# A gated recurrence of 512 steps: the direct x products moved into step 0, the block products moved by one step

## The chip, the cores and the metric

The kernel runs on one core of one Trainium2 chip. The time is the device time of one execution in microseconds, from the core's first instruction to its last with what the runtime lays around it; the shown runs of the kernel before took 1656.86, 1657.39 and 1657.92 us (median 1657.39). The core has a matrix engine (PE, with weight loads as a row of their own, PEld), a vector engine (DVE), an activation engine (ACT), a general engine (POOL) and a queue that issues transfers (SP).

## The reference

Eight sequences of 512 steps and 512 features go through a gated recurrence, and the input is added to its result. For each step t, with a state `h` of 8 x 512:

```python
fused = sigmoid(concat([x_t, h]) @ w_W + w_b)
hidden_state, output_state = split(fused, 2)
memory_state = x_t @ wx_W + wx_b + hidden_state * (h @ wh_W + wh_b)
h = output_state * h + (1 - output_state) * tanh(memory_state)
out[t] = x_t + h
```

Everything is float32. Of each step's products the part with `x_t` (512 x 1536) doesn't depend on the state and can be done at any time before the step; the part with `h` (512 x 1536) can only start when the step before is done.

## The kernel before, in words

**Layout.** The 512 features are cut into four parts of 128; a matmul takes 128 rows of the contraction and writes 32 rows of PSUM (tile "128*32"), so that four matmuls, j = 0 to 3, fill the 128 rows of a bank. Weights are moving operands: `wx` (x part), `wa` and `wb` (state part).

**A step** (one turn of the loop over i, 0 to 511). The state's halves lie in `hTA` (parts k = 0, 1) and `hTB` (k = 2, 3). PE adds the state's products to three banks: A (192 columns: gate r, gate z and the inner product h of half A), B (128) and C (64, in the tile `cs`). The order is the string `ORDER` for all steps but the first, which has `FIRST`; an `x` in it stands for a fourth of a group's x products. When A is complete DVE transposes it (`tr`, `md1A`, `tz`), ACT applies the sigmoids, DVE's scans form the memory, ACT its tanh, and DVE's next scans (`update`) write the new `hTA`; with B and C the same happens for half B. After C, PE does x products that belong to later steps, until the new `hTA` lets the next step's A begin.

**Groups and blocks.** Four steps are a group, two groups a block of eight steps; u = 0 to 7 is a step's place in its block. The x products of groups 0 to 3 are done directly by `prefill` (16 matmuls of 384 columns a group, one part of four matmuls for each k), into `xps[0]` (even groups) or `xps[1]` (odd groups), which `seed` has filled with the bias. From the third block on, the x products of a block are done as seven smaller products (P1 to P7 and a copy E of P5) of sums of weights (`tw`, made by `weight_sum` on DVE) and of sums of x (`sx`, made by `x_sum` on POOL). `x_step` hands out their columns: `SHARE[u]` columns at place u, 384 or 288, in the order of `SLOTS`. The registers AL, BE, GA, DE (halves of `xps`) and `eps` take the products; ACT and DVE copy and add them into `even` and `odd`, from which `spread` (ACT) fills the banks A, B, C of the group and `turn_x` (DVE) its part of `md1`. All of that is written at the end of a step, after its updates, and runs on ACT and DVE while PE does the next step's A.

**The order** of every engine's instructions is that of the program text; a queue waits in front of the instruction whose semaphore isn't there yet. Two banks of each name alternate between groups.

**Around step 0.** SP issues `wx` in four transfers, `wa` in four, `wb` in two, then the second half of x chunk 0 (`load_x(0, 1)`) and chunks 1 to 3. PE does group 0, then a matmul of zeros over `xps[1]` (`warm`), then step 0, whose A products are added onto `xps[0]` itself. DVE's order there is two weight sums of 128 x 1536, then `turn_x(0)`, then step 0's transposes.

Of the kernel before, what the change touches and what calls it, by code (L numbers as in the profile page):

```python
# [16 lines left out]
B = 8  # L17
# [7 lines left out]

ORDER = "A0 B0 A1 A2 A3 B1 B2 B3 C0 C1 C2 C3"

FIRST = "A0 x A1 x A2 x A3 B0 B1 B2 B3 C0 C1 C2 C3"

BANKS = {"A": 192, "B": 128, "C": 64}  # L30

# [22 lines left out]
def tile_cond_rnn_residual(  # L54
# [70 lines left out]
    def load_x(c, half=slice(0, 2)):  # L125

        if c < NCH:
            if c not in xins:
                xins[c] = xin_p.tile([P, 2, NQ, TC * B // 2], F32, tag="xin", name=f"xin_{c}")
            nc.sync.dma_start(  # L130
                out=xins[c][:, half], in_=x[c].rearrange("p (e k n) -> p e k n", e=2, k=NQ)[:, half]
            )
# [18 lines left out]
    wa = const.tile([P, NQ, NQ, 192], F32, name="wa")  # L151
    for k in range(NQ):
        nc.sync.dma_start(out=wa[:, k], in_=wa_d[k])
    wb = const.tile([P, NQ, NQ, 192], F32, name="wb")
    nc.sync.dma_start(out=wb[:, :3], in_=wb_d)
    nc.sync.dma_start(out=wb[:, 3], in_=wb3_d)
# [4 lines left out]
    load_x(0, 1)  # L161

    def pair(n, name, rows, slots):

# [51 lines left out]
    def mm(out_, lhsT, rhs, start=False):  # L216
        nc.tensor.matmul(  # L217
            out_, lhsT, rhs, start=start, stop=False, skip_group_check=True
        )
# [4 lines left out]
    def warm():  # L224

        mm(xps[1], zeros[:, :128], zeros)
# [25 lines left out]
    def seed(g):  # L252

        nc.scalar.copy(xps[g % 2], bias)  # L254

    def prefill(g):

        c, t0 = divmod(g * GS, TC)
        for k in range(NQ):
            for j in range(NQ):  # L260
                mm(
                    xps[g % 2][32 * j : 32 * j + 32, XC],
                    x_of(c, k, t0, GS),
                    wx[:, k, j, :],
                )
            yield
# [5 lines left out]
    def spread(g, names):  # L272

        for n in names:
            nc.scalar.copy(banks[g % 2][n], source(g)[:, XP[n]])

    def turn_x(g, hf):

        c0 = XP["X"].start + HU * hf
        nc.vector.transpose(  # L280
            md1[hf][g % 2][:, :, :, 1].rearrange("p n c -> p c n"), source(g)[:, c0 : c0 + HU]
        )
# [11 lines left out]
    def weight_sum(n, k=slice(0, 2), j=slice(0, 2)):  # L294

        a, b = [
            (wx_of(0, 1), wx_of(0, 0)),
            (wx_of(1, 1), tw[0]),
            (wx_of(1, 1), wx_of(0, 1)),
            (wx_of(1, 0), tw[1]),  # L300
        ][n]
        nc.vector.tensor_tensor(tw[n][:, k, j], a[:, k, j], b[:, k, j], ALU.subtract)
# [55 lines left out]
    weight_sum(0)  # L358
    spread(0, "BCA")
    for hf in range(2):  # L360
        turn_x(0, hf)

    pool_done = {}
    for i in range(T):
# [7 lines left out]

        for n in (ORDER if i else FIRST).split():
            if n == "x":
                take(first[1], 1)
                continue
            bank, k = n[0], int(n[1])
            hs = hT[k // 2][i % NH][:, :, k % 2, 2]
            for j in range(NQ):
                to = ps[bank] if i or bank != "A" else xps[0][:, XP["A"]]  # L380
                mm(to[32 * j : 32 * j + 32, :], hs, wh(bank, k, j))
# [87 lines left out]
        if i == 0:  # L469

            seed(2)
# [16 lines left out]
        o, u = divmod(i, 2 * GS)  # L488
        nxt, two = o + 1 < NG // 2, o + 2 < NG // 2
        if i == 0:  # L490
            nc.scalar.copy(odd[:, XC], xps[1][:, XC])
        if u == 0:
            spread(2 * o + 1, "AC")
            turn_x(2 * o + 1, 0)
            turn_x(2 * o + 1, 1)
        elif u == 1:
            if o and nxt:
                nc.vector.tensor_tensor(reg(GA), reg(BE), more[HI], ALU.add)
                nc.scalar.copy(even[LO, XC], reg(AL))
            spread(2 * o + 1, "B")  # L500
        elif u == 2:
            if o == 0:
                nc.scalar.copy(even[:, XC], xps[0][:, XC])
                seed(3)
            elif nxt:
# [4 lines left out]
        elif u == 3:  # L510
            if two:
                nc.scalar.copy(reg(AL), bias[LO, XC])
                x_sum(o + 2, 0)
        elif u == 4:
            if o == 0:
                nc.scalar.copy(odd[:, XC], xps[1][:, XC])
            elif nxt:
# [3 lines left out]
        elif u == 5 and nxt:  # L521
            if o:
                nc.scalar.copy(odd[LO, XC], reg(GA))
            spread(2 * o + 2, "A")
            turn_x(2 * o + 2, 0)
        elif u == 6 and nxt:
            spread(2 * o + 2, "BC")
            turn_x(2 * o + 2, 1)
            if two:
                nc.scalar.copy(more[HI], eps)  # L530
                x_sum(o + 2, 1)
        elif u == 7 and nxt:
            if two:
                nc.scalar.copy(reg(BE), reg(AL))
                nc.scalar.copy(both[LO], reg(DE))
                x_sum(o + 2, 3)
        if 1 <= i < 9:
            weight_sum(1 if i < 5 else 3, *divmod((i - 1) % 4, 2))
        if i == 2:
# [102 lines left out]
```

## Time and profile before

| | |
|---|---|
| time, median of 3 runs | 1657.39 us |
| profiled execution: its time, its span | 1659.38 us, 1657.43 us |
| mean granted TensorE clock | 0.999 |
| matmul records | 54253 |
| busy: PE, PEld, DVE, ACT, POOL | 1645.1, 1487.9, 1152.0, 1198.4, 303.2 us |
| moved by DMA | 31.16 MB |

PE's busy time counts pipelined matmuls whose ends are modelled, so a busy share of 99% doesn't say that PE has no slack; it is read from the distance between matmuls. One matmul of the program appears as two records in the trace, so "x8" is four matmuls. The bank A of step 0 is called xp in the trace of before, since it is the tile `xps[0]`. The start of a step is the first row `A<-wa,hTA`, or the row `tr<-A` of DVE, the first reader of a complete A.

### The profile page before, as it was taken

How to read it: one execution, taken by the hardware profiler on the slowest of the kernel's cores; microseconds unless marked ns; L12 is line 12 of the kernel's file. 1: busy time of each engine (PE TensorE's matmuls, PEld its weight loads, DVE VectorE, ACT ScalarE, POOL GpSimd, SP SyncE). 2: the span in 40 equal slices, each digit the busy share in tenths (PEclk: the TensorE clock that was granted, in tenths of full speed). 3: DMA queues.
4: the chain of work that ended last, by engine and by line, in shares of the span. 5: the costliest groups of instructions: out<-in, count | busy, mean ns of one | idle time of the engine just before them, and what ended most of it. 6: DMA issues, size and time to landing. Idle time of an engine off the chain costs nothing.

```text
span 1657.4 us, 126070 instructions
## 1 busy us (share of the span) xinstructions
PE 1645.1 (99%) x54253; PEld 1487.9 (90%) x54253; DVE 1152.0 (70%) x9193; ACT 1198.4 (72%) x6009; POOL 303.2 (18%) x1283
## 2 busy tenths in 40 slices
PE   8999999999999999999999999999999999999998
PEld 5999999999888889999999999999999999989987
DVE  5776676676766766767667667676676676766766
ACT  4777777777777777777777777777777777777775
POOL 1211111111111111111111111111111111111111
PEclk9999999999999999999999999999999999999999
DMA  4000000000000000000000000000000000000000
GB/s 182 11 14 17 15 14 15 17 15 14 14 16 16 14 14 16 16 14 14 16 16 14 15 16 16 15 14 16 16 15 14 16 16 15 14 16 11 10 10 10
DMA packets 37287, 31.16 MB, mean 19 GB/s; under 512 B 4084, under 2 KB 35060, under 8 KB 36600
## 3 DMA queue, kind: packets, MB, share of 16 engines
q1 hardware_dynamic: 36576, 22.95, 4.5%
q8 instruction: 424, 6.95, 1.7%
q14 instruction: 135, 1.11, 0.2%
q10 hardware_dynamic: 152, 0.16, 0.0%
HBM read 14.70 MB, written 8.39 MB: 14 GB/s over the span
## 4 chain that ended last, share of the span: by engine, by line
PE 98%; DVE 1%; DMA 1%; issue 0%; ACT 0%; SPq 0%
PE A L217 40%; PE B L217 26%; PE xp L217 17%; PE cs L217 13%; PE eps L217 1%; DMA wx<-in_wx_dram 1%; DVE tr L407 0%; DVE m L391 0%; DVE tz L407 0%; DVE md1B L423 0%; DVE hTA L391 0%; DVE md1A L423 0%; SPq L149 0%; ACT hTB L246 0%; ACT xp L254 0%
## 5 line engine op out<-in xcount | busy, mean ns | idle before, releaser
L217 PE MATMUL A<-wa,hTA 128*32 128x192 f32 x8176 | 547.6, 326 | 2.1 <-DVE hTA L391 2.1
L217 PE MATMUL A<-wa,hTB 128*32 128x192 f32 x8176 | 440.7, 326 | 0.0
L217 PE MATMUL B<-wb,hTA 128*32 128x128 f32 x8192 | 440.6, 273 | 0.0
L217 PEld LDWEIGHTS A<-wa,hTA 128*32 128x32 f32 x8176 | 281.3, 122 | 129.8 <-DVE hTA L391 103.7
L407 DVE STREAM_TRANSPOSE tr<-A 128x64 f32<-128x64 f32 x511 | 127.6, 250 | 369.4 <-PE A L217 369.4
L545 POOL TENSOR_TENSOR ot<-xin,hTB 128x16 f32<-128x16 f32 x503 | 125.9, 250 | 1309.3 <-DVE hTB L391 989.0
L217 PEld LDWEIGHTS B<-wb,hTA 128*32 128x32 f32 x8192 | 337.5, 122 | 5.7
L217 PEld LDWEIGHTS A<-wa,hTB 128*32 128x32 f32 x8176 | 323.0, 122 | 13.0 <-DVE hTB L391 0.4
L217 PE MATMUL B<-wb,hTB 128*32 128x128 f32 x8192 | 332.2, 273 | 0.0
L217 PE MATMUL xp<-tw,sx 128*32 128x96 f32 x1488 | 267.5, 433 | 0.0
L217 PEld LDWEIGHTS B<-wb,hTB 128*32 128x32 f32 x8192 | 255.1, 122 | 0.0
L246 ACT ACTIVATE md0A<-tr 128x16 f32<-128x16 f32 x512 | 112.3, 219 | 191.3 <-DVE tr L407 177.4
L391 DVE TENSOR_TENSOR_SCAN hTB<-hd0B,hTB 128x24 f32<-128x24 f32 x1024 | 157.8, 195 | 100.5 <-ACT hTB L246 100.5
L217 PE MATMUL cs<-wb,hTA 128*32 128x64 f32 x8192 | 222.9, 219 | 0.0
L217 PE MATMUL cs<-wb,hTB 128*32 128x64 f32 x8192 | 222.8, 219 | 0.0
L217 PE MATMUL xp<-wx,xin 128*32 128x384 f32 (+2 forms) x1304 | 219.6, 425 | 0.0
L217 PEld LDWEIGHTS cs<-wb,hTA 128*32 128x32 f32 x8192 | 200.4, 122 | 0.0
L391 DVE TENSOR_TENSOR_SCAN hTA<-hd0A,hTA 128x24 f32<-128x24 f32 x1024 | 190.1, 186 | 0.0
L246 ACT ACTIVATE hd0B<-tz 128x16 f32<-128x16 f32 x512 | 116.0, 227 | 93.3 <-DVE tz L407 93.3
L246 ACT ACTIVATE hTB<-hTB 128x16 f32<-128x16 f32 x512 | 120.1, 234 | 78.9 <-DVE hTB L391 53.1
L217 PEld LDWEIGHTS cs<-wb,hTB 128*32 128x32 f32 x8192 | 173.0, 122 | 0.0
L246 ACT ACTIVATE hTA<-m 128x8 f32<-128x8 f32 x1024 | 160.6, 206 | 2.8 <-DVE m L391 0.5
(105 smaller groups left out, 2664.3 us busy)
## 6 DMA issues: line engine op xcount, KB each, us to landing
out_dram<-ot SPq DMA_DIRECT2D x128, 64.0 KB, 1.6
xin<-in_x_dram SPq DMA_DIRECT2D x112, 64.0 KB, 2.2
wx<-in_wx_dram SPq DMA_DIRECT2D x4, 768.0 KB, 6.9
wa<-in_wa_dram SPq DMA_DIRECT2D x4, 384.0 KB, 8.9
wb<-in_wb_dram SPq DMA_DIRECT2D x1, 1152.0 KB
xin<-in_x_dram SPq DMA_DIRECT2D x3, 256.0 KB, 8.3
wb<-in_wb_dram SPq DMA_DIRECT2D x1, 384.0 KB, 11.2
head<-in_xh_dram ACTq DMA_DIRECT2D x1, 144.0 KB, 4.9
```

The source lines that it names most:

```text
L217: nc.tensor.matmul(out_, lhsT, rhs, start=start, stop=False, skip_group_check=True)
L246: inst = nc.scalar.activation(out_, in_, func, **kw).ins
L391: return nc.vector.tensor_tensor_scan(*[t_[:, :, c_].rearrange("p n c s -> p (n c s)") for t_ in (out_, d0, d1)], 0.0, ALU.mult, ALU.add,).ins
L407: inst = nc.vector.transpose(t_.rearrange("p c n -> p (c n)"), raw[n][hf]).ins
L545: return engine.tensor_tensor(ot[:, t, 2 * hf : 2 * hf + 2, :].rearrange("p c n -> p n c"), x_of(c, slice(2 * hf, 2 * hf + 2), t, 1).rearr ...
```

## The change

- `FIRST`: in step 0 the four A parts come first, then four x parts, then B and C. The x parts are those of group 2, not of group 1.
- All of group 1 is done before the loop, where the `warm` matmul stood. Step 0's A goes to the bank A, not to `xps[0]`; `spread(0)` copies A first.
- Group 3 is done one part a step in steps 1 to 4; before, groups 2 and 3 were done two parts a step there.
- `weight_sum(2)` stands behind `turn_x(0)`, and `weight_sum(0)` in step 0 between the first half's memory scans and `turn_r(1)`. The seeds of groups 2 and 3 and the copy of group 1 into `odd` stand ahead of the loop.
- The second half of x chunk 0 is issued ahead of `wb`, not behind it.
- The block products start at place u = 5 of the block two before theirs, not at 4: `SHARE` and the sums and copies at the end of each step are turned by one place. Exceptions: `more<-eps` moves from u = 6 to u = 1 of the next block, `spread(2o+1, "AC")` from 0 to 1 and its "B" from 1 to 2, `spread(2o+2)` from A at 5 and BC at 6 to AB at 6 and C at 7, `turn_x(2o+1)` stays at u = 0.

```diff
-FIRST = "A0 x A1 x A2 x A3 B0 B1 B2 B3 C0 C1 C2 C3"
+FIRST = "A0 A1 A2 A3 x x x x B0 B1 B2 B3 C0 C1 C2 C3"
-SHARE = [384, 384, 384, 288, 288, 288, 288, 384]
+SHARE = [384, 384, 384, 384, 288, 288, 288, 288]
...
+    load_x(0, 1)
     wb = const.tile([P, NQ, NQ, 192], F32, name="wb")
...
-        at = sum((SHARE * 2)[4 : u if u > 3 else u + 8]) - SHARE[4] // 3
-        o += 2 if u > 3 else 1
+        at = sum((SHARE * 2)[5 : u if u > 4 else u + 8]) - SHARE[5] // 3
+        o += 2 if u > 4 else 1
...
     take(prefill(0))
-    warm()
-    first = {g: prefill(g) for g in (1, 2, 3)}
-    weight_sum(2)
-    weight_sum(0)
-    spread(0, "BCA")
+    take(prefill(1))
+    first = {g: prefill(g) for g in (2, 3)}
+    spread(0, "ABC")
     for hf in range(2):
         turn_x(0, hf)
+    weight_sum(2)
+    seed(2)
+    nc.scalar.copy(odd[:, XC], xps[1][:, XC])
+    seed(3)
...
-                take(first[1], 1)
+                take(first[2], 1)
...
-        if i < 5:
-            take(first[(i + 3) // 2], 2)
-        if i > 3:
+        if 1 <= i < 5:
+            take(first[3], 1)
+        if i > 4:
             x_step(*divmod(i, 2 * GS))
...
-        pa = ps["A"] if i else xps[0][:, XP["A"]]
+        pa = ps["A"]
...
         memory(0, 1)
+        if i == 0:
+            weight_sum(0)
         turn_r(1)
...
         if u == 0:
-            spread(2 * o + 1, "AC")
+            if o == 0:
+                spread(1, "A")
+            if sums:
+                nc.scalar.copy(reg(BE), reg(AL))
+                nc.scalar.copy(both[LO], reg(DE))
+                x_sum(o + 1, 3)
             turn_x(2 * o + 1, 0)
             turn_x(2 * o + 1, 1)
         elif u == 1:
-            if o and nxt:
+            if sums:
+                nc.scalar.copy(more[HI], eps)
+            spread(2 * o + 1, "BC" if o == 0 else "AC")
```

PE from the end of group 0 to the B products of step 0, as a difference (`xp_183` is `xps[0]`, `xp_184` is `xps[1]`, `A_179` the first A bank; `head` holds x of groups 0 and 1, `xin` the second half of chunk 0):

```order
-L217 MATMUL xp_184<-zeros 128x512
-L217 MATMUL xp_183<-wa,hTA_90 32x192 x4
-L217 MATMUL xp_184<-wx,head 32x384 x4
-L217 MATMUL xp_183<-wa,hTA_90 32x192 x4
-L217 MATMUL xp_184<-wx,head 32x384 x4
-L217 MATMUL xp_183<-wa,hTB_98 32x192 x4
-L217 MATMUL xp_184<-wx,head 32x384 x4
-L217 MATMUL xp_183<-wa,hTB_98 32x192 x4
+L217 MATMUL xp_184<-wx,head 32x384 x16
+L217 MATMUL A_179<-wa,hTA_90 32x192 x8
+L217 MATMUL A_179<-wa,hTB_98 32x192 x8
+L217 MATMUL xp_183<-wx,xin_85 32x384 x16
```

Sixteen matmuls of group 1 stand ahead of step 0's first A product, and sixteen of group 2 between its A and B products.

DVE from the head of the loop to the transposes for half B in step 0, first before (`tw_161` and `tw_159` are two of the summed weights):

```order
L302 TENSOR_TENSOR tw_161<-wx 128x1536
L302 TENSOR_TENSOR tw_159<-wx 128x1536
L280 STREAM_TRANSPOSE md1A_110<-xp_183 128x64
L280 STREAM_TRANSPOSE md1B_112<-xp_183 128x64
L407 STREAM_TRANSPOSE tr_0_294<-xp_183 128x64
```

and now:

```order
L280 STREAM_TRANSPOSE md1A_110<-xp_183 128x64
L280 STREAM_TRANSPOSE md1B_112<-xp_183 128x64
L302 TENSOR_TENSOR tw_161<-wx 128x1536
L408 STREAM_TRANSPOSE tr_0_311<-A_179 128x64
L424 STREAM_TRANSPOSE md1A_110<-A_179 128x64
L408 STREAM_TRANSPOSE tz_0_315<-A_179 128x64
L434 MEMSET idle 128x1
L392 TENSOR_SCALAR m_0_309<-md0A_106,md1A_110 128x16 x2
L302 TENSOR_TENSOR tw_159<-wx 128x1536
L408 STREAM_TRANSPOSE tr_0_324<-B_180 128x64
```

The readers of `xps[0]` no longer stand behind the two weight sums, and the second of these stands inside step 0 (scans appear as TENSOR_SCALAR here).

ACT between the last state copy of one step and the first sigmoid of the next, at the place with the most copies: before at u = 6,

```order
L246 ACTIVATE hTB_105<-hTB_105 128x8x2
L275 COPY B_180<-even 128x128
L275 COPY cs<-even 128x64
L530 COPY more<-eps 64x384
L246 ACTIVATE md0A_107<-tr_39_3895 128x2x8
```

and now at u = 1:

```order
L246 ACTIVATE hTB_100<-hTB_100 128x8x2
L504 COPY more<-eps 64x384
L275 COPY A_181<-odd 128x192
L275 COPY cs<-odd 128x64
L246 ACTIVATE md0A_106<-tr_42_4160 128x2x8
```

The copy of `eps` stands with the spread of another group, 192 and 64 columns in place of 128 and 64.

More of the change, by code (lines that the diff above doesn't have):

```diff
@@ L159, in wh @@
         return wa[:, k, j] if bank == "A" else wb[:, k, j, {"C": slice(0, 64), "B": slice(64, 192)}[bank]]
-    load_x(0, 1)
     def pair(n, name, rows, slots):
@@ L379, in tile_cond_rnn_residual @@
             for j in range(NQ):
-                to = ps[bank] if i or bank != "A" else xps[0][:, XP["A"]]
-                mm(to[32 * j : 32 * j + 32, :], hs, wh(bank, k, j))
-        if i < 5:
-            take(first[(i + 3) // 2], 2)
-        if i > 3:
+                mm(ps[bank][32 * j : 32 * j + 32, :], hs, wh(bank, k, j))
+        if 1 <= i < 5:
+            take(first[3], 1)
+        if i > 4:
             x_step(*divmod(i, 2 * GS))
@@ L468, in tile_cond_rnn_residual @@
         tc.add_manual_dep(update(0, 1), r_done[1].name, SYNC)
-        if i == 0:
-            seed(2)
         if i == T - 1:
@@ L490, in tile_cond_rnn_residual @@
         if i == 0:
-            nc.scalar.copy(odd[:, XC], xps[1][:, XC])
+            nc.scalar.copy(even[:, XC], xps[0][:, XC])
+        sums = o > 0 and nxt
         if u == 0:
-            spread(2 * o + 1, "AC")
+            if o == 0:
[4 more added lines that the diff above has]
+                x_sum(o + 1, 3)
             turn_x(2 * o + 1, 0)
@@ L496, in tile_cond_rnn_residual @@
         elif u == 1:
-            if o and nxt:
+            if sums:
+                nc.scalar.copy(more[HI], eps)
+            spread(2 * o + 1, "BC" if o == 0 else "AC")
+        elif u == 2:
+            if sums:
                 nc.vector.tensor_tensor(reg(GA), reg(BE), more[HI], ALU.add)
                 nc.scalar.copy(even[LO, XC], reg(AL))
[L500 to L505, printed above, removed]
+            if o:
+                spread(2 * o + 1, "B")
+        elif u == 3:
+            if sums:
                 nc.vector.tensor_tensor(odd[HI, XC], reg(GA), both[LO], ALU.add)
@@ L509, in tile_cond_rnn_residual @@
                 x_sum(o + 2, 2)
-        elif u == 3:
+        elif u == 4:
+            if o == 0:
+                nc.scalar.copy(odd[:, XC], xps[1][:, XC])
             if two:
@@ L513, in tile_cond_rnn_residual @@
                 x_sum(o + 2, 0)
[L514 to L517, printed above, removed]
+        elif u == 5:
+            if sums:
                 nc.vector.tensor_tensor(even[HI, XC], reg(BE), both[HI], ALU.add)
@@ L520, in tile_cond_rnn_residual @@
                 nc.scalar.copy(reg(DE), step_bias[HI])
-        elif u == 5 and nxt:
+        elif u == 6 and nxt:
+            spread(2 * o + 2, "AB")
+            turn_x(2 * o + 2, 0)
+        elif u == 7 and nxt:
             if o:
                 nc.scalar.copy(odd[LO, XC], reg(GA))
[L524 to L527, printed above, removed]
+            spread(2 * o + 2, "C")
             turn_x(2 * o + 2, 1)
             if two:
-                nc.scalar.copy(more[HI], eps)
                 x_sum(o + 2, 1)
[L532 to L536, printed above, removed]
         if 1 <= i < 9:
```

## The prediction

> **What bounds the kernel now.** I read the page's busy times and chain first, then the distances between matmuls (timeline of PE), since a busy share of a pipelined engine doesn't show slack, and last the first 22 us engine by engine.
>
> ```profile
> PE 1645.1 (99%) x54253; PEld 1487.9 (90%) x54253; DVE 1152.0 (70%) x9193; ACT 1198.4 (72%) x6009; POOL 303.2 (18%) x1283
> PE 98%; DVE 1%; DMA 1%; issue 0%; ACT 0%; SPq 0%
> ...
> 47.64 0.55 PE L217 MATMUL A<-wa,hTA 128*32 128x192 f32 x8
> 50.26 0.49 PE L217 MATMUL xp<-wx,xin 128*32 128x384 f32 x2
> 50.91 0.55 PE L217 MATMUL A<-wa,hTA 128*32 128x192 f32 x8
> 57.44 0.55 PE L217 MATMUL A<-wa,hTA 128*32 128x192 f32 x8
> 60.54 0.55 PE L217 MATMUL A<-wa,hTA 128*32 128x192 f32 x8
> ...
> 1644.38 0.55 PE L217 MATMUL A<-wa,hTA 128*32 128x192 f32 x8 [0.23 <-DVE hTA L391]
> 1647.46 0.55 PE L217 MATMUL A<-wa,hTA 128*32 128x192 f32 x8 [0.24 <-DVE hTA L391]
> ```
>
> Step starts give three lengths. A step's state products take 47.64 to 50.26, 2.62 us. With 384 columns of block products the step is 3.27 us (47.64 to 50.91), with 288 it is 3.10 (57.44 to 60.54), without any 3.08 (1644.38 to 1647.46): there PE waits for the new state, 0.46 us in all. So up to 0.46 us of x products are free in a step, and every microsecond above that is paid in full. Steps with products are bound by PE, the last steps by the chain through DVE and ACT.
>
> The start is another matter. PE there, with what DVE does beside it:
>
> ```profile
> 11.15 0.85 PE L217 MATMUL xp<-wx,head 128*32 128x384 f32 x8 [0.48 <-DMA wx<-in_wx_dram]
> 11.94 1.13 PE L217 MATMUL xp<-zeros 128*128 128x512 f32 x2
> 15.05 0.86 PE L217 MATMUL xp<-wa,hTA 128*32 128x192 f32 x8 [1.99 <-issue]
> ...
> 19.66 0.52 PE L217 MATMUL xp<-wa,hTB 128*32 128x192 f32 x8
> 19.99 0.64 PE L217 MATMUL B<-wb,hTA 128*32 128x128 f32 x16
> 20.86 0.42 PE L217 MATMUL cs<-wb,hTA 128*32 128x64 f32 x16
> ...
> 21.31 0.84 PE L217 MATMUL xp<-wx,head 128*32 128x384 f32 x8
> 21.95 0.52 PE L217 MATMUL A<-wa,hTA 128*32 128x192 f32 x8
> 11.23 3.43 DVE L302 TENSOR_TENSOR tw<-wx 128x1536 f32<-128x1536 f32 x2 [2.01 <-DMA wx<-in_wx_dram]
> 14.74 0.21 DVE L280 STREAM_TRANSPOSE md1B<-xp 128x64 f32<-128x64 f32 x1
> ```
>
> Step 0's A begins at 15.05, 0.10 us after the second transpose of `xps[0]` ends (14.95). That transpose stands behind two weight sums of 3.43 us, and A adds onto the tile which it reads: DVE's order holds PE, not a load. The loads agree:
>
> ```profile
> 3.03 3.46 SPq L153 DMA_DIRECT2D wa<-in_wa_dram  x4
> DMA to landing us min/median/max: 8.3/8.9/9.4
> 7.37 0.33 SPq L156 DMA_DIRECT2D wb<-in_wb_dram  x1
> wb<-in_wb_dram SPq DMA_DIRECT2D x1, 384.0 KB, 11.2
> 9.27 4.03 SPq L130 DMA_DIRECT2D xin<-in_x_dram  x4
> xin<-in_x_dram SPq DMA_DIRECT2D x1, 128.0 KB, 9.7
> ```
>
> The first part of `wa` lands by 3.03 + 9.4 = 12.43 at the latest, the fourth, whose issue ends at 6.49, by 14.8 with the shortest time of that row, 15.4 with its median and 15.9 with the longest; the last of `wb` at 18.57; the x half at 18.97.
>
> Behind the gap PE is slow. Mean clock granted (the column behind the busy time), a microsecond a row:
>
> ```profile
> core 0: us, PE busy (x), PEclk, DMA share, GB/s
> 15.00:16.00 1.00, 0.95 (x12) 0.56 1.00 424
> 16.00:17.00 1.00, 1.00 (x12) 0.50 0.93 393
> 17.00:18.00 1.00, 1.00 (x16) 0.50 0.94 376
> 18.00:19.00 1.00, 1.00 (x16) 0.73 1.06 398
> ```
>
> The missing shares add up to 0.44 + 0.50 + 0.50 + 0.27 = 1.71 us of PE time. The same from the matmuls: at full clock four matmuls of 384 columns take 21.31 to 21.95, 0.645, and four of 192 columns 19.66 to 19.99, 0.325. A with three x parts is 4 x 0.325 + 3 x 0.645 = 3.24; it took 15.05 to 19.99, 4.94.
>
> **The change, part by part.**
>
> *Group 1 ahead of the loop, `warm` and the gap gone.* Group 0's last part begins at 11.15 and ends its work at 11.80. Group 1 needs nothing new (x in `head`, `wx` complete): 4 x 0.645 = 2.58, to 14.38. A now goes to the bank A and waits for one copy by ACT, over by then, and for `wa`: to 14.38 + 1.30 = 15.68. Its fourth part is wanted at 15.36; the longest landing, 15.9, would cost 0.5, the median, 15.4, costs nothing, and I take the median. PE is busy from 11.15 on, so I expect no half clock.
>
> *Group 2 between A and B.* It needs `seed(2)` on ACT, which waits for `turn_x(0)` on DVE, now free at about 12.1 (two transposes of 0.21 us each, as in the row at 14.74, then one copy of 512 columns, which I bound by twice the 0.47 us of 384 columns in the second rival's rows): ready by 14. It needs the x half, now issued ahead of `wb`: 128 KB at about 410 GB/s (last column above) is 0.31 us behind `wa`, so 15.7 with the median and 16.2 with the longest landing, against 15.68. It takes 2.58, to 18.26. In exchange `wb` is 0.31 us later: its last part takes the place of the x half, 18.97. B's last four matmuls want it at 18.26 + 0.65 = 18.91. I price that at 0.1; at worst, `wb` half a microsecond late, 0.5. B 0.87, C 0.45: C ends at 19.68.
>
> *Weight sums.* One takes half of 3.43, 1.72. The first stands at about 12.6 to 14.4 and A's first transpose comes at 15.9. The second begins when half A's scans are done, some 0.8 us behind that (16.8), and ends at 18.5; half B's transposes can't start before B is complete, 19.2. Both lie beside group 2 and cost nothing; if group 2 weren't there, the second would hold `update(0, 0)` and so step 1 by about 1.7.
>
> *Step 1 to 5.* With nothing between C and the next A step 0 closes like the last steps, with 0.46 of waits: step 1 starts at 20.14. Steps 1 to 4 do 2.62 + 0.645 = 3.27 each: step 5 starts at 33.22. Before:
>
> ```profile
> 33.97 0.51 PE L217 MATMUL A<-wa,hTA 128*32 128x192 f32 x8
> 35.74 0.25 DVE L407 STREAM_TRANSPOSE tr<-A 128x64 f32<-128x64 f32 x1 [0.78 <-PE A L217]
> 39.95 0.25 DVE L407 STREAM_TRANSPOSE tr<-A 128x64 f32<-128x64 f32 x1 [1.63 <-PE A L217]
> ```
>
> A step's first transpose comes 35.74 - 33.97 = 1.77 behind its start, so step 5 started at 39.95 - 1.77 = 38.18. Step 4 took 4.21: half a group (1.29) and the first 192 columns of E (0.32). These columns go into step 5, where 0.32 is under the free 0.46, so that step takes 3.08.
>
> *All other steps.* From step 6 on step i does what step i - 1 did. The products end one step later, so of the last steps at 3.08 one is lost, and step 5 is the one gained: zero. Sums and copies keep their distance to the products, or have more; they are hidden behind the next step's A as before, but for the place in the second rival.
>
> Sum: 38.18 - 33.22 = 4.96 us. The same by terms: from 11.80 to 15.05 nothing was done but `warm`, 3.25; half clock 1.71; E 0.32; in steps 1 to 4 of before 0.27 of waits (38.18 - 21.95 = 16.23, against 4 x 3.91 + 0.32); less the 0.46 at the end of step 0 and the 0.1 for `wb`. Group 2's 2.58 us only change their place: into a stretch that starts that much earlier. The span 1657.43 becomes 1652.5. The profiled execution took 1659.38, its median unprofiled 1657.39; I take the difference over: 1657.39 - 4.96 = 1652.4.
>
> **The clock, by row and by rule.** The rows show half clock from 15.1 to about 18.5 after PE had stood for 1.99 us. The Trainium skill (TensorE: Matmul & The Clock Gate, Part 1) says that the clock is judged in free-running windows of about 3.4 us and falls after an idle one, and that where the window lies changes from run to run. The half clock's length agrees with this; that 1.99 us of standing were enough does not agree with an idle window of 3.4. If the rule were strict, the timed runs of before would not have had the half clock, and the sum would be 4.96 - 1.71.
>
> **Rivals.**
>
> *The timed runs had no half clock, or less of it.* What is lost depends on how much work falls on it, from nothing to 1.71. For it: one profile alone shows it, and the three times lie 1.06 us apart. Against: that spread is under 1.71, and the standing is the same in every run. Without it the gain is 3.25: 1654.1.
>
> *Slower: ACT is late at u = 1.* Now `more`, A and C are copied there between the last state copy and the next sigmoid. Rows of the nearest places:
>
> ```profile
> 709.25 0.47 ACT L530 COPY more<-eps 64x384 f32<-64x384 f32 x1
> ...
> 711.79 0.23 ACT L246 ACTIVATE hTB<-hTB 128x16 f32<-128x16 f32 x1 [0.15 <-DVE idle L543]
> 712.05 0.45 ACT L534 COPY xp<-xp 64x384 f32<-64x384 f32 x1
> 712.53 0.48 ACT L535 COPY both<-xp 64x384 f32<-64x384 f32 x1
> 713.19 0.22 ACT L246 ACTIVATE md0A<-tr 128x16 f32<-128x16 f32 x1 [0.18 <-DVE tr L407]
> ...
> 715.31 0.32 ACT L275 COPY A<-odd 128x192 f32<-128x192 f32 x1
> 715.57 0.21 ACT L275 COPY cs<-odd 128x64 f32<-128x64 f32 x1
> ```
>
> The two copies at u = 7, also a step of 384 columns, take 0.93 and leave 0.18. The new three take 0.47 + 0.32 + 0.21 = 1.00 and leave about 0.11. An overrun would stretch 62 blocks: it eats the whole gain from 4.96/62 = 0.08 us beyond the slack, and decides for slower by 0.2% from 0.13. At 0.15 the time is 1652.4 + 9.3 = 1661.7. For it: it is the fullest place. Against: all durations are measured.
>
> *The gap was a load's.* Were the first A held by `wa` until 15.05, group 1 would still fill most of it, A would end 0.67 later: 1653.1. Against: 12.43 above.
>
> *Loads late in step 0* (x half 0.5, `wb` 0.5): up to 0.9 less, 1653.3.
>
> **The numbers.** Forecast 0.60, no or little half clock 0.18, loads (both cases) 0.10, ACT late or another wait in every block 0.09, else 0.03. A difference of 0.2% (3.3 us) is about what a measurement of this kernel can tell from none. Faster by more: forecast, loads and half the clock rival, 0.79; within: 0.12; slower: 0.09. The range reaches from 1651.4 (the sum with 1 us for the spread of the runs) to 1654.9 (the clock rival with a late load): 0.85 of the cases; the forecast's own is 1651.9 to 1653.0.
>
> **What would show it.** The clock stays at 1.00 from 15 on; the first A starts near 14.4, step 1 near 20.1; B waits for a DMA at most briefly; DVE's second weight sum ends before B does; the last matmuls of a block keep 3.27 and 3.10, four of each. The forecast is wrong if PE shows waits for `xp` or the banks in every block, if the clock is halved elsewhere in the first 20 us, or if B starts past 19.

## The result and the profile after

| | before | after |
|---|---|---|
| time, median of 22 runs each | 1657.88 us (1656.83 to 1660.06) | 1655.01 us (1654.41 to 1655.94) |
| ratio, 95% interval | | 0.998 (0.9975 to 0.9986) |
| profiled execution: time, span | 1659.38 us, 1657.43 us | 1654.89 us, 1652.9 us |
| start of the span to the first transpose of step 8 | 49.43 us | 45.54 us |
| from there to that of step 500 | 1568.99 us | 1568.33 us |
| from there to the end | 39.0 us | 39.07 us |

Faster by 2.87 us, where 4.96 were forecast; 1655.0 lies 2.6 us above the forecast and just above the upper end of its range, 1654.9. The kernel before took 0.49 us more here than the 1657.39 that the forecast started from: as a gain the range is 2.5 to 6.0 us, and 2.87 lies inside it. The last three rows of the table cut the profiled spans at the first transposes of steps 8 and 500: nearly all of the change is at the start, and 3.89 us are gained there.

PE in the profile after, from the end of group 0 to step 1 (start, busy time of the group, idle time before it and who ended it):

```profile
11.19 3.43 PE L217 MATMUL xp<-wx,head 128*32 128x384 f32 x40 [0.32 <-DMA wx<-in_wx_dram]
14.44 0.83 PE L217 MATMUL A<-wa,hTA 128*32 128x192 f32 x16
15.09 0.83 PE L217 MATMUL A<-wa,hTB 128*32 128x192 f32 x16
15.74 2.76 PE L217 MATMUL xp<-wx,xin 128*32 128x384 f32 x32
18.32 0.62 PE L217 MATMUL B<-wb,hTA 128*32 128x128 f32 x16
18.75 0.40 PE L217 MATMUL B<-wb,hTB 128*32 128x128 f32 x8
20.27 0.44 PE L217 MATMUL B<-wb,hTB 128*32 128x128 f32 x8 [1.12 <-DMA wb<-in_wb_dram]
...
21.31 0.55 PE L217 MATMUL A<-wa,hTA 128*32 128x192 f32 x8
```

Up to 18.75 this is the forecast with 0.06 us added: A at 14.44 instead of 14.38, group 2 at 15.74 instead of 15.68, B at 18.32 instead of 18.26. Then B's last four matmuls stand for 1.12 us until the last part of `wb` lands, and step 1 begins at 21.31, not at 20.14. The chain of waits names the transfer (start, duration):

```profile
9.30 10.92 DMA wb<-in_wb_dram
20.23 0.04 issue
20.27 0.49 PE B L217 x8
```

It was issued at 9.30, where the kernel before issued the x half (9.27), and took 10.92 us; the x half had taken 9.7 there. The clock, in rows of a microsecond, is whole:

```profile
core 0: us, PE busy (x) PEld busy (x) DVE busy (x) ACT busy (x) POOL busy (x), PEclk, DMA share, GB/s
15.00:16.00 1.00, 1.00 (x28) 0.75 (x24) 0.01 (x1) 0.81 (x2) 0.00 (x0) 1.00 1.04 442
16.00:17.00 1.00, 1.00 (x16) 0.39 (x12) 0.99 (x7) 0.69 (x4) 0.00 (x0) 1.00 1.02 433
17.00:18.00 1.00, 1.00 (x17) 0.39 (x12) 1.00 (x1) 0.06 (x1) 0.00 (x0) 1.00 0.92 367
18.00:19.00 1.00, 1.00 (x32) 0.72 (x24) 0.45 (x1) 0.00 (x0) 0.00 (x0) 1.00 0.99 374
19.00:20.00 1.00, 0.15 (x8) 0.00 (x0) 0.00 (x0) 0.00 (x0) 0.00 (x0) 1.00 1.05 403
```

DVE's first transposes of steps 1, 4, 5 and 6 give the step lengths:

```profile
23.21 0.25 DVE L408 STREAM_TRANSPOSE tr<-A 128x64 f32<-128x64 f32 x1 [0.34 <-PE A L217]
...
33.00 0.25 DVE L408 STREAM_TRANSPOSE tr<-A 128x64 f32<-128x64 f32 x1 [0.47 <-PE A L217]
36.27 0.25 DVE L408 STREAM_TRANSPOSE tr<-A 128x64 f32<-128x64 f32 x1 [0.68 <-PE A L217]
39.35 0.25 DVE L408 STREAM_TRANSPOSE tr<-A 128x64 f32<-128x64 f32 x1 [0.49 <-PE A L217]
```

Step 1 to 4 is 9.79, so 3.26 a step; the step with the first columns of E takes 3.08. In the blocks the steps are 3.265 and 3.105 us, four of each, as before. ACT at u = 1, the place of the second rival:

```profile
714.07 0.47 ACT L504 COPY more<-eps 64x384 f32<-64x384 f32 x1
714.57 0.32 ACT L275 COPY A<-odd 128x192 f32<-128x192 f32 x1
714.83 0.21 ACT L275 COPY cs<-odd 128x64 f32<-128x64 f32 x1
715.21 0.22 ACT L246 ACTIVATE md0A<-tr 128x16 f32<-128x16 f32 x1 [0.18 <-DVE tr L408]
```

The three copies leave 0.18 us ahead of the sigmoid (0.11 was forecast); nothing is late.

### The profile page after: what moved, and what is told of

It reads as the page before. It is cut to its first block, busy times and chain, and to the rows that moved or that the text cites. A ratio compares the mean times of both kernels' runs of the same rounds, so it can differ in the third digit from the quotient of the medians.

```text
span 1652.9 us, 126068 instructions
## 1 busy us (share of the span) xinstructions
PE 1642.6 (99%) x54251; PEld 1456.2 (88%) x54251; DVE 1153.7 (70%) x9193; ACT 1199.8 (73%) x6009; POOL 303.1 (18%) x1283
## 3 DMA queue, kind: packets, MB, share of 16 engines
HBM read 14.70 MB, written 8.39 MB: 14 GB/s over the span
## 4 chain that ended last, share of the span: by engine, by line
PE 98%; DMA 1%; DVE 1%; issue 0%; SPq 0%; ACT 0%
PE A L217 40%; PE B L217 27%; PE xp L217 17%; PE cs L217 13%; DMA wb<-in_wb_dram 1%; PE eps L217 1%; DMA wx<-in_wx_dram 0%; DVE tr L408 0%; DVE m L392 0%; DVE md1B L424 0%; DVE hTA L392 0%; DVE tz L408 0%; DVE md1A L424 0%; SPq L149 0%; ACT hTB L246 0%
## 5 line engine op out<-in xcount | busy, mean ns | idle before, releaser
L217 PE MATMUL A<-wa,hTA 128*32 128x192 f32 x8192 | 536.9, 326 | 2.0 <-DVE hTA L392 1.9
L217 PE MATMUL B<-wb,hTA 128*32 128x128 f32 x8192 | 427.6, 273 | 0.0
L217 PEld LDWEIGHTS A<-wa,hTA 128*32 128x32 f32 x8192 | 269.3, 122 | 134.8 <-DVE hTA L392 108.6
L217 PEld LDWEIGHTS B<-wb,hTA 128*32 128x32 f32 x8192 | 319.0, 122 | 18.4 <-DMA wb<-in_wb_dram 0.2
L217 PEld LDWEIGHTS A<-wa,hTB 128*32 128x32 f32 x8192 | 309.3, 122 | 24.8 <-DVE hTB L392 0.2
L217 PE MATMUL B<-wb,hTB 128*32 128x128 f32 x8192 | 326.0, 273 | 1.1 <-DMA wb<-in_wb_dram 1.1
L217 PEld LDWEIGHTS B<-wb,hTB 128*32 128x32 f32 x8192 | 248.4, 122 | 1.4 <-DMA wb<-in_wb_dram 1.4
L217 PE MATMUL cs<-wb,hTB 128*32 128x64 f32 x8192 | 216.5, 219 | 0.0
L217 PE MATMUL cs<-wb,hTA 128*32 128x64 f32 x8192 | 216.3, 219 | 0.0
L217 PEld LDWEIGHTS cs<-wb,hTA 128*32 128x32 f32 x8192 | 193.9, 122 | 0.0
## 6 DMA issues: line engine op xcount, KB each, us to landing
wb<-in_wb_dram SPq DMA_DIRECT2D x1, 384.0 KB, 10.9
```

The lines of the kernel that those rows point to most:

```text
L217: nc.tensor.matmul(out_, lhsT, rhs, start=start, stop=False, skip_group_check=True)
```

## The experiments

They are in three series, each with its own runs of the kernel before: 1659.44 us (median of 32, 1657.29 to 1661.6), 1662.32 (33 runs, of which one took 2465.38 and the others 1658.81 to 1664.65) and 1661.98 (22 runs, 1660.52 to 1663.49). A ratio is to the kernel before of the same series; times of different series are not compared. Names that start with a are edits of the changed kernel, with b of the kernel before.

### The changed kernel again, twice

> The changed kernel once more, as the base of this set. If its short gain is settled in the program (an instruction fetch that falls into the load of wb at the same place in each run), the last part of wb lands near 20.2 us again, PE stands about 1.1 us ahead of B's last part and the clock stays whole. If it was chance, the landing lies elsewhere, between 18.9 and 20.2, and the span is up to 1.2 us shorter.

1655.74 us (10 runs, 1655.02 to 1656.69), ratio 0.9976 (0.9967 to 0.9986). Here B did not stand:

```profile
14.70 0.83 PE L217 MATMUL A<-wa,hTA 128*32 128x192 f32 x16
...
18.58 0.62 PE L217 MATMUL B<-wb,hTA 128*32 128x128 f32 x16
19.01 0.72 PE L217 MATMUL B<-wb,hTB 128*32 128x128 f32 x16
...
20.33 0.55 PE L217 MATMUL A<-wa,hTA 128*32 128x192 f32 x8
```

and, in the view of the tile `wb`,

```profile
L157 SPq DMA_DIRECT2D wb<-in_wb_dram x1: 327/327/327, 9.6 to 9.6; - x1
DMA to landing us min/median/max: 9.7/10.1/10.6
```

From the first A to step 1 it took 20.33 - 14.70 = 5.63, against the 5.76 of the forecast (14.38 to 20.14) and the 6.87 of the profile above. The last part of `wb` was issued at 9.6 and landed 9.7 later, at some 19.3. So the same program runs both with and without the wait. The span, 1653.2 us, was not shorter for it: at step 8 this run was 0.98 us ahead of the profile above, and from there to step 500 it took 1.26 us more. The two traces differ in one more thing around that time: a transfer of 16 KB of instructions. Of the transfers of the profile after, from 17.5 to 18.6 us, then of this run, from 18.5 to 19.6, then of the kernel before, from 20 to 21 (queue, packets, MB, share of the engines):

```profile
q8 instruction: 1, 0.02, 5.3%
```

```profile
q8 instruction: 1, 0.02, 5.3%
```

```profile
q8 instruction: 1, 0.02, 6.6%
```

5.3% of 16 engines over 1.1 us is one engine for about 0.93 us. In the profile after, its start (17.54) lies within the load of `wb`, and after it the last packets of `wb` come one by one, as on a single engine, to 19.8 us; in this run it starts at 18.57, when all but six of `wb`'s packets have moved, in the kernel before at 20.16, when `wb` is there.

> The changed kernel once more, as the partner of the next two. The theory (gain = gap and half clock of the start, less what wb's late part and the missing half clock of some runs take away) expects a ratio to the kernel before of 0.9972 to 0.9986, as in its two earlier series (0.9981 and 0.9976). In its profile either the first instruction fetch behind 16 us comes before 17.9 us, and then B's last matmuls of step 0 wait 0.7 to 1.2 us for wb, with step 0 to step 1 at 7.0 to 7.3 us; or it comes later, and then they wait less than 0.2 us, with 5.9 to 6.1 us. If the fetch has nothing to do with it, the two go together in no such way.

1658.39 us (10 runs, 1657.07 to 1659.89), ratio 0.9977 (0.9968 to 0.9987). B stood for 1.31 us, with the fetch at 17.60: the kind of run that the expectation names, but longer than its 0.7 to 1.2, and step 0 to step 1 took 7.40, over its 7.0 to 7.3. Over all profiles of this study:

```
kernel      first fetch behind 16 us   start of B's last part   idle ahead of it
a_fill2           17.35                      20.14                0.0 (two x parts stand there)
a_fill1           17.48                      20.27                0.39 (one x part stands there)
b_dve             17.53                      20.11                1.51
after             17.54                      20.27                1.12
a_act             17.60                      20.12                1.00
a_again2          17.60                      20.33                1.31
a_fillc           17.62                      20.40                0.49 (one x part stands there)
a_norot2          17.68                      20.16                1.04
a_norot           17.76                      20.24                0.86
a_again           18.57                      19.30                below 0.1
a_act2            18.60                      19.26                below 0.1
a_headx           18.80                      19.72                0.0
before            20.16                      20.64                0.0
b_busy            20.17                      19.02                0.0
```

Where the fetch starts by 17.76, B's last part starts at 20.1 to 20.4, whatever is put ahead of it; where it starts from 18.57 on, the part waits less than 0.1. All 14 agree, and the pattern was written down ahead of the last four (a_again2, a_norot2, a_fillc, a_act2). It ties the wait to the fetch; it is not an experiment on it, since no kernel moved the fetch alone. The number of fetches points to PE: the profile's page of before counts 54253 records of matmuls and as many weight loads, 108506 in all, against 424 fetches, so one comes per 256 of them, and in each trace the fetches lie 255.9 to 256.1 of them apart on the average. By the first fetch PE had started 273 of them in the profile after, and 227 in that of before, 2.6 us later. That doesn't set its place alone, for it was 363 in b_busy (at 20.17). Why the same program has it at 17.5 in some executions and at 18.6 in others stays open.

### The x half behind wb

```diff
-    load_x(0, 1)
     wb = const.tile([P, NQ, NQ, 192], F32, name="wb")
...
+    load_x(0, 1)
...
-                    x_of(c, k, t0, GS),
+                    x_of(c, k, GS if g == 2 else t0, GS),
```

So that group 2 needs no late x it multiplies the x of group 1 in place of its own.

> The x half is loaded behind wb again, and group 2 multiplies group 1's x from the first load instead of its own, so that nothing but wx and wa lies ahead of wb. Theory queue position: the last part of wb was late because of what stood ahead of it, so it lands as before, near 18.6, B doesn't wait, C ends near 19.6, and the time is 1.2 us under the changed kernel's. Theory fetch: one DMA engine loses the 0.93 us of an instruction fetch (16 KB, at 17.54 us in the changed kernel, at 20.16 before) while wb is under way; then wb gains only the 0.31 us of the 128 KB and lands near 19.9, and the time is 0.3 us shorter.

1656.04 us (1654.67 to 1656.72), ratio 0.9976 (0.9968 to 0.9985). `wb` landed 11.2 us after its issue at 8.16, at 19.35 with the fetch at 18.80, between the 18.6 and the 19.9 of the two theories, and B did not wait; but neither did the unedited kernel of that series in its profile, so this run doesn't tell the order of the two loads from the fetch. The timed runs are no faster than those of the unedited kernel (1655.74).

### x products ahead of B's last part

```diff
-FIRST = "A0 A1 A2 A3 x x x x B0 B1 B2 B3 C0 C1 C2 C3"
+FIRST = "A0 A1 A2 A3 x x x x B0 B1 B2 y B3 C0 C1 C2 C3"
...
-            yield
+                yield
...
-            if n == "x":
-                take(first[2], 1)
+            if n in "xy":
+                take(first[2 if n == "x" else 3], 4)
...
-            take(first[3], 1)
+            take(first[3], 3)
```

One part of group 3 (a `y`) is done while `wb` is awaited, and steps 1 to 4 do three matmuls each instead of four. The second kernel has `y y` and two matmuls a step.

> One part of group 3 (four matmuls, 0.645 us) goes in front of B's last part in step 0, where PE stood 1.1 us, and steps 1 to 4 do three matmuls each (2.62 + 0.48 = 3.10 in place of 3.27). If the stand is there in every run, the part costs nothing and the time falls by 4 x 0.16 = 0.64 us under the changed kernel's. If the stand was chance, 0.645 is paid and 0.64 gained: no difference.

1656.34 us (1655.26 to 1658.01), ratio 0.9983 (0.9974 to 0.9991). The wait fell to 0.39, but B's last part still began at 20.27, and the steps didn't shrink: 23.20 to 26.46 and on to 29.73, 3.26 each:

```profile
20.27 0.44 PE L217 MATMUL B<-wb,hTB 128*32 128x128 f32 x8 [0.39 <-DMA wb<-in_wb_dram]
```

In the profile the work was hidden in the wait, and nothing was returned: of four matmuls with j = 0 to 3, which write separate rows of the bank, leaving out one saves 0.01 us a step. The timed runs lie 0.60 above a_again's. With nothing returned, the part costs 0.65 where `wb` is on time and nothing where it is late, so this looks more like `wb` on time in most of them; but the runs spread over 2.75 us, and it is a hint.

> Two parts of group 3 (1.29 us) in front of B's last part in step 0, two matmuls in each of steps 1 to 4 (2.62 + 0.32, under the free 0.46: 3.08 us). If wb is late by 1.3 us in every run, they are free there, and the time is 4 x 0.185 = 0.74 us under the changed kernel's; if wb comes at 18.97, 1.29 is paid and the kernel is 0.55 us longer.

1659.57 us (1657.6 to 1662.81), ratio 0.9985 (0.9976 to 0.9994). Both parts fit ahead of B's last part, which starts at 20.14 without a wait, and the steps with two matmuls took 3.264, 3.175, 3.332 and 3.243 us: two cost nearly what four cost.

So the third kernel cuts columns, not matmuls: one part ahead of B's last part, and the other 1152 columns as 288 a step with all four j.

```diff
+    def columns(g, at, end):
+        c, t0 = divmod(g * GS, TC)
+        while at < end:
+            k, c0 = divmod(at, W)
+            c1 = min(W, c0 + end - at)
+            for j in range(NQ):
+                mm(...)
+            at += c1 - c0
...
+            if n == "y":
+                columns(3, 0, W)
+                continue
...
-            take(first[3], 1)
+            columns(3, W + 288 * (i - 1), W + 288 * i)
```

> One part of group 3 stands ahead of B's last part, where wb is waited for, and steps 1 to 4 do the other 1152 columns as 288 each, with all four j. If wb is late in most of the timed runs, this fills 0.65 of the wait, and steps 1 to 4 take 3.105 instead of 3.265: 0.64 us below a_again2. If wb is on time in the timed runs, the 0.65 is paid in step 0 and returned in steps 1 to 4: the same time. The profile shows steps 1 to 4 at 3.10 to 3.12 in both cases.

1657.81 us (7 runs, 1656.65 to 1661.11), against 1658.39 for the unedited kernel of the same series; ratio 0.9977 (0.9966 to 0.9988). Now the steps shrink:

```profile
23.33 0.25 DVE L425 STREAM_TRANSPOSE tr<-A 128x64 f32<-128x64 f32 x1 [0.36 <-PE A L217]
26.43 0.25 DVE L425 STREAM_TRANSPOSE tr<-A 128x64 f32<-128x64 f32 x1 [0.52 <-PE A L217]
29.54 0.25 DVE L425 STREAM_TRANSPOSE tr<-A 128x64 f32<-128x64 f32 x1 [0.52 <-PE A L217]
32.95 0.25 DVE L425 STREAM_TRANSPOSE tr<-A 128x64 f32<-128x64 f32 x1 [0.45 <-PE A L217]
36.05 0.25 DVE L425 STREAM_TRANSPOSE tr<-A 128x64 f32<-128x64 f32 x1 [0.51 <-PE A L217]
```

3.10 and 3.11 (the third has another 0.30, in which PE stood for nothing that the profile shows). The medians differ by 0.58 (the means by 0.22) where a late `wb` gave 0.64 and a punctual one 0, but each scatters by more; this doesn't settle how often `wb` is late in the timed runs.

### The turn by one place undone

The start as in the changed kernel; `SHARE`, products, sums and copies as in the kernel before (the rest of the diff shown above, backwards).

```diff
-SHARE = [384, 384, 384, 384, 288, 288, 288, 288]
+SHARE = [384, 384, 384, 288, 288, 288, 288, 384]
...
-        if i > 4:
+        if i > 3:
             x_step(*divmod(i, 2 * GS))
```

> The start of the changed kernel with the block products, sums and copies at their places of before (first products in step 4). By the prediction the turn by one place is worth only E's 192 columns in step 4: 0.32 us longer than the changed kernel, steps 4 at 3.59 us, and the steady steps at 3.27 and 3.10, four of each. The rival: the turned copies cost or spare something in each of 62 blocks; then the sum of eight steady steps differs from the changed kernel's 25.50 us, and 0.02 us there is 1.2 us of the whole.

1657.24 us (1656.39 to 1659.05), ratio 0.9986 (0.9978 to 0.9995); 1.5 us above the unedited kernel of its series, where 0.32 was the price of E. Its profile had the 0.32 alone (step 4 of 3.57) and the same steady steps, so it was run again.

> The changed start with products, sums and copies at the places of before, once more: its first series gave a time 1.5 us above the changed kernel's, where the sum has 0.32 us for the 192 columns of E that come back into step 4. If 0.32 is right, the time is 0.3 us above that of a_again2 with the scatter of such means, so 0 to 1.0 us above; if the turn by one place is worth more than the 0.32, the difference is again 1.2 to 2 us, and then some steady step must be longer in the profile than 3.265 or 3.105. Step 4 takes 3.57 to 3.60, with every other step as in the changed kernel.

1659.07 us (11 runs, 1656.9 to 1660.82), ratio 0.9982 (0.9973 to 0.9991); 0.68 above the unedited kernel. Steps 3 to 5 begin, by their transposes,

```profile
29.62 0.25 DVE L408 STREAM_TRANSPOSE tr<-A 128x64 f32<-128x64 f32 x1 [0.68 <-PE A L217]
32.88 0.25 DVE L408 STREAM_TRANSPOSE tr<-A 128x64 f32<-128x64 f32 x1 [0.47 <-PE A L217]
36.45 0.25 DVE L408 STREAM_TRANSPOSE tr<-A 128x64 f32<-128x64 f32 x1 [0.98 <-PE A L217]
```

so step 4 takes 3.57, 0.30 more than the 3.27 in the changed kernel, and step 5 another 0.03. The blocks keep 3.265 and 3.105, four of each. The turn is worth those 0.33 in the profiles; the timed differences of 1.5 and 0.68 lie above that, and no step of the blocks accounts for the rest. Stands of PE scattered over steps 8 to 500, for which the profile shows no cause, add up to 1.0 and 1.4 us more in these two profiles than in a_again and a_again2. Whether that is chance or a price of the old places stays open.

### One part of the gap at a time, on the kernel before

Two more `warm` matmuls, so that PE hardly stands:

```diff
-    warm()
+    for _ in range(3):
+        warm()
```

> The kernel before with two more matmuls of zeros behind warm, 0.85 us each, so that PE is busy until about 14.5 us and stands about 0.5 us, not 2, ahead of step 0. Nothing else moves. If the half clock is what the standing costs, the granted clock stays 1.00 behind 15 us and the span is 1.71 us under that of a run with the full half clock (1657.4 to 1655.7). If the timed runs of before lost only part of it, as their spread of 3.2 us and the gain of 2.9 in place of 4.5 say, their median falls by about 1.0 to 1.2 us, towards the fastest runs of before, and the spread shrinks to that of the changed kernel, 1.5 us. If the timed runs never had it, the median stays.

1662.35 us (1659.73 to 1663.99), ratio 1.0 (0.9991 to 1.0009). The half clock is gone:

```profile
16.00:17.00 1.00, 1.00 (x20) 0.65 (x16) 0.00 (x0) 0.00 (x0) 0.00 (x0) 1.00 0.95 402
17.00:18.00 1.00, 1.00 (x20) 0.65 (x16) 0.00 (x0) 0.00 (x0) 0.00 (x0) 1.00 0.95 380
```

and the first transpose of step 0 came at 18.63 instead of 20.25, 1.62 earlier, close to the 1.71 of the sum. All 11 runs of it had a mean clock of 1.000, where 17 of the 32 of the kernel before (without the one of 2465.38) had 0.999 or less: so the standing brings the half clock, not in each run, and one profile alone couldn't have shown it. The time didn't follow: the step from 1 to 2 took 4.285 instead of 3.834, and another 5.64 us (1.2 in the first profile of before) went into scattered stands of PE between steps 8 and 500. Its runs are on average 0.79 us shorter than those of before with 0.999, as forecast in kind, but 0.85 longer than those with 1.000; what the two matmuls cost there stays open. As a price of the half clock in the timed runs this is inconclusive: the interval of the ratio reaches 1.5 us to both sides.

Then DVE's order alone: the weight sums moved as in the change, nothing else.

```diff
-    weight_sum(2)
-    weight_sum(0)
...
+    weight_sum(2)
...
+        if i == 0:
+            weight_sum(0)
```

> The kernel before with DVE's order alone changed: turn_x of group 0 ahead of the weight sums, the second of which goes into step 0. If DVE's order made the gap, A starts near 13.1 in place of 15.05, with no half clock, and then B waits for wb (about 17.6 and 18.6); C ends near 19.3 and step 1 starts near 20.0, 2.0 us earlier than in the profile of before; steps 1 to 4 as before. In timed runs, which lose part of the half clock, 1.0 to 1.5 us under before. If the gap was a load's, A still starts near 15.

1661.85 us (1659.57 to 1663.94), ratio 0.9998 (0.9989 to 1.0007).

```profile
13.20 0.55 PE L217 MATMUL xp<-wa,hTA 128*32 128x192 f32 x8
...
17.72 0.66 PE L217 MATMUL B<-wb,hTA 128*32 128x128 f32 x16 [1.06 <-DMA wb<-in_wb_dram]
18.19 0.40 PE L217 MATMUL B<-wb,hTB 128*32 128x128 f32 x8
20.11 0.44 PE L217 MATMUL B<-wb,hTB 128*32 128x128 f32 x8 [1.51 <-DMA wb<-in_wb_dram]
```

The first transposes of steps 0 and 1, in the kernel before and in this one:

```profile
20.25 0.25 DVE L407 STREAM_TRANSPOSE tr<-xp 128x64 f32<-128x64 f32 x1 [5.30 <-PE xp L217]
24.08 0.24 DVE L407 STREAM_TRANSPOSE tr<-A 128x64 f32<-128x64 f32 x1
```

```profile
16.71 0.25 DVE L406 STREAM_TRANSPOSE tr<-xp 128x64 f32<-128x64 f32 x1 [1.98 <-PE xp L217]
23.58 0.25 DVE L406 STREAM_TRANSPOSE tr<-A 128x64 f32<-128x64 f32 x1
```

A starts at 13.20 instead of 15.05, so it was DVE's order that held it, and no load: the third rival falls. And the gap hid the load of `wb`: with the gap gone, B stands for it, 1.06 and 1.51 us, and of the 3.54 us gained at the first transpose of step 0 (16.71 instead of 20.25) 0.50 is left at that of step 1 (23.58 instead of 24.08), where 2.0 were expected. (These idle times count from modelled ends. From start to start the two waits cost 1.28 and 1.70 us, nearly all of the 3.04 lost.)

### ACT later at u = 1

An extra copy of 192 columns on ACT in every block, then, in a second kernel, two (384 and 192 columns):

```diff
             if sums:
+                nc.scalar.copy(extra, odd[:, XP["A"]])
```

> The changed kernel with one more copy on ACT at u = 1 of each block from the second on (192 columns, 0.32 us, into a tile that nobody reads). The changed kernel's profile shows ACT idle for about 0.18 us there. By the second rival's rule the copy overruns by 0.14 us, stretches 62 blocks by that and makes the kernel 8 to 9 us slower than the changed one. If PE's products hide part of it, less.

1659.53 us (1658.01 to 1662.59), ratio 0.9986 (0.9977 to 0.9995). The copy took 0.35 and the sigmoid came late:

```profile
717.85 0.25 DVE L409 STREAM_TRANSPOSE tr<-A 128x64 f32<-128x64 f32 x1 [1.13 <-PE A L218]
717.97 0.35 ACT L508 COPY extra<-odd 128x192 f32<-128x192 f32 x1
...
718.23 0.22 ACT L247 ACTIVATE md0A<-tr 128x16 f32<-128x16 f32 x1
```

0.38 after the transpose's start instead of 0.28 (714.93 to 715.21 in the profile after), so 0.10 late, at no cost in the step: its median stays 3.265. No unedited kernel was timed in this series; the 8 to 9 us of the second rival's price are not there, since the ratio lies 0.0006 to 0.001 above those of the changed kernel in its own series, 1.0 to 1.7 us.

> Two more copies on ACT at u = 1, of 384 and 192 columns, 0.80 us in all, ahead of the copies that stand there. The slack ahead of the first sigmoid was 0.18 us in the profile. By the price of the second rival (every overrun is paid in 62 blocks) the step at u = 1 grows by 0.62 us and the time by 38 us. By the reading of the run with one extra copy (a step of 384 columns has another 0.19 us, its distance from the 3.08 us of a step that waits) it grows by about 0.43, to 3.65 to 3.72, and the time by 24 to 28 us. If ACT has still more room there, less than 15 us.

1683.65 us (one run), 25.3 above the unedited kernel of its series.

```profile
726.78 0.25 DVE L409 STREAM_TRANSPOSE tr<-A 128x64 f32<-128x64 f32 x1 [1.13 <-PE A L218]
...
727.71 0.22 ACT L247 ACTIVATE md0A<-tr 128x16 f32<-128x16 f32 x1
...
728.70 0.38 PE L218 MATMUL A<-wa,hTA 128*32 128x192 f32 x4 [0.20 <-DVE hTA L393]
...
730.50 0.25 DVE L409 STREAM_TRANSPOSE tr<-A 128x64 f32<-128x64 f32 x1 [0.30 <-PE A L218]
```

The sigmoid is 0.93 behind the transpose, 0.65 late; the step takes 730.50 - 726.78 = 3.72, 0.46 longer. The other 0.19 is what a step with 384 columns has above one without products, 3.265 - 3.08. Over 62 blocks 0.46 is 28.5 us; the profiled span is 24.0 above that of the unedited kernel, which lost 1.1 more up to step 8, where B stood for 1.31, and whose steady steps hold 3.2 us more of scattered stands.

## Why the prediction was right or wrong

- **Group 1 ahead of the loop, the gap and `warm` gone (3.25): right.** A begins 0.06 after the forecast, and DVE's order alone brings A to 13.20, so the cause was the one named.
- **The half clock (1.71): right in the profile, too large for the timed runs.** The clock is whole after the change, and in the kernel before it is whole when PE is kept busy. But the sum was made against one profiled execution of 1659.38 us, which two of the 22 runs above exceed, and taken whole from the median. In the three later series, the runs of before with a mean clock of 0.999 or less were on average longer than those of 1.000 by 1.40, 1.64 and 1.07 us (15 against 17 runs, 17 against 15, 8 against 14). So at most about half of the runs had it, and their mean gains some 0.4 to 0.9, not 1.71. This is the first rival, half true, which the prediction had as a case apart and not as a share in the forecast. The class is not a pure one: in the profile of a_again2 the 0.999 came from the last two microseconds, where PE does nothing, and of the 138 runs of all kernels but the one before 24 have 0.999 or less too. The rule of the Trainium skill (TensorE: Matmul & The Clock Gate, Part 1) that the window's place changes from run to run agrees with the two classes; its strict form, in which an idle window is needed, doesn't agree with the half clock of the profile after 1.99 us.
- **wb (0.1, at worst 0.5): the step that failed.** "Its last part takes the place of the x half, 18.97." In a_again it nearly did so, 9.7 after its issue, at 19.25, and PE stood for under 0.1. In eight of the eleven profiles with the new start it landed at 20.0 to 20.4, and PE stood for 0.9 to 1.3 where nothing was put ahead of it. The size taken from the x half's row was that of an undisturbed load. What it lacked, as far as the 14 profiles tell, is the fetch of instructions, which in the profile of before lay at 20.16, behind `wb`. Why the fetch comes into the load now is not shown; it did so with DVE's order alone (b_dve, 17.53), and did not in b_busy (20.17).
- **Group 2 between A and B, the weight sums, steps 1 to 5, E: right.** 2.58 for group 2; the second weight sum runs from 16.71 to 18.45, ahead of the first transpose of B; steps of 3.265 and one of 3.08. E is worth 0.30 to 0.33.
- **All other steps, zero: right in the steps.** 3.265 and 3.105, four of each, in both kernels. In the timed runs the old places cost 1.5 and 0.68, where the 0.33 of E is accounted for; the rest stays open.
- **The second rival: wrong in its price, right to be unlikely.** An overrun at u = 1 isn't paid from the first nanosecond. From 0.18 us of idle time and 0.19 of the step it takes 0.37 us of more work on ACT before anything is paid, then in each of 62 blocks.
- **Loads late in step 0:** this rival was the right place, at up to 0.5 for `wb` and a chance of 0.10 with the third rival together; the place needed both more chance and a larger price. The upper end of the range, the clock rival with a late load, is 1654.1 and 0.9, which makes 1655.0 and not 1654.9. And the terms add up to 4.99, where the difference of the step starts is 4.96.

The account, an estimate: 4.96, less 1.0 for the half clock that half of the runs or more don't have, less some 0.7 for `wb` (about 1.0 in eight of eleven profiles), is 3.3. The medians of the three series that hold the kernel as it is gave 2.87, 3.70 and 3.59. That the timed runs have the late `wb` as often as the profiles is an assumption: of the tests of it in timed runs, the x half behind `wb` shows nothing, one part ahead of B's last part points to a `wb` on time (0.60 longer), the same with fewer columns to a late one (0.58 shorter), and all are small against the scatter. So the two terms are the ones that were too large; how the missing 1.3 to 2.1 us divide between them stays open.

## What to carry to other kernels

When a gap at the start is closed, list what it hid: here PE's gap covered the last load, and DVE's order alone, which closed the gap, left 0.50 of 3.54 us at the next step and nothing that the timed runs could show. A term read from one profiled execution must be checked against that execution's place among the timed runs before it is taken whole from their median. Slack at a place is the idle time seen there plus what the step has above its chain of waits; on a full engine both must be used up before an overrun is paid.

## What the runs showed of the hardware

- Instructions were fetched in transfers of 16 KB, each 0.9 to 1.8 us long, 424 in an execution of 512 steps, one per 256 matmuls and weight loads of PE. In the changed kernel the last part of `wb` took 10.9 and 11.1 us from issue to landing when a fetch began at 17.5 to 17.6, within that load, and 9.7 when it began at 18.57, near the load's end.
- A standing time of PE of 1.99 us was followed by half clock over the next 3.4 us in the profile of before. With 0.27 us of it (b_busy) there was none, nor with the 1.51 us of b_dve. In the timed runs at most half of those of the kernel before show it (40 of 86 with a mean clock of 0.999 or less).
- Of four matmuls that write four separate groups of 32 rows, leaving out one or two saved 0.01 us a step on the average of four steps. Taking a quarter of the columns from all four saved 0.16.
- PE stands now and then for 0.05 to 0.8 us with nothing in the profile that it waits for. Some steps have it in several profiles (step 286 in seven of the fourteen), most in one or two. Summed over steps 8 to 500 this was 0.3 to 7 us in the profiles of this study, more than most of the terms of the prediction; what causes it stays open.
